# Layernorms in pairs of tiles, pieces paced by an estimate of VectorE's time, and one transfer fewer at the end, in a two-layer model kernel

## The chip, the cores and the metric

The kernel runs on one core of one Trainium2 chip. Five engines of that core matter: TensorE (PE in the profile) multiplies matrices, VectorE (DVE) and ScalarE (ACT) do elementwise work, GpSimd (POOL) does elementwise work and issues some transfers, SyncE (SP) issues the other transfers. The metric is the device time of one launch in microseconds (us); less is better.

## The reference

The input `x` is 4 x 1024 tokens of 256 numbers. Four blocks follow one another, each added to `x` behind a layernorm. All of it is float32.

```python
x = x + _layernorm(_L0_attn_ref(_layernorm(x), ...))   # gated attention in groups of 64
x = x + _layernorm(_L0_ffn_ref(_layernorm(x), ...))    # low-rank feed-forward
x = x + _layernorm(_L1_attn_ref(_layernorm(x), ...))   # 16 heads of 16, relu weights, own layernorm
x = x + _layernorm(_L1_ffn_ref(_layernorm(x), ...))    # experts choose their tokens
```

The two last ones are where the change lies:

```python
# _L1_attn_ref(x): H = 16 heads, HD = 16
w   = relu(q @ k.T / sqrt(HD))
out = (w / (sum(w) + 1e-6)) @ v
y   = x + out @ w_out + b_out
return (y - mean(y)) * rsqrt(var(y) + 1e-5) * gamma + beta
# _L1_ffn_ref(x): 8 experts, each takes the 1024 tokens with the highest gate
S    = sigmoid(xt @ Wg).T
G, I = top_k(S, 1024)
out  = (gelu(xt[I] @ W1 + b1) @ W2 + b2) * G[..., None]
new_x = zeros.at[I].add(out)
```

So one token passes four layernorms in the L1 attention: the one ahead of the projections (tag `a` in the code), the block's own with `gamma` and `beta` (tag `b`), the one around the block (tag `c`), and the one ahead of the experts' gate (tag `g`).

## The kernel before

The 4096 tokens are cut into 8 blocks of 512 (t = 0 to 7), and a block into 4 tiles of 128 tokens by 256 numbers. `xs[t]` keeps `x` of a block in on-chip memory for the whole run. The stages are the L0 layers (to 428 us), the L1 attention (428 to 1078), its tail up to the gate's logits (to 1108), the choice of tokens, the experts (1159 to 1637), and the last layernorm with its addition (to the end).

**L1 attention.** Two blocks make a row of 1024 tokens (b = 0 to 3); qh says which half of the row gives the queries. For each half there are 4 groups of heads by 8 tiles of keys, 256 steps in all. A step is `scores` (four matmuls into two single buffers and one pair buffer; relu of the singles on ACT, L1226, and of the pair on DVE, L1227) and then, from the step before, `weigh` (L1233, four matmuls that add up in `po`). The order on PE, DVE and ACT is the program's, written out by hand. Behind `weigh` stands `go_on`, which lets other work in: it takes one entry of the list `beside` (matrix work: projections of the next row, turning, output projection, gate) if there is one, and one piece of the list `rest` (vector work), two if `beside` gave something, none in the last step of a group.

**Pieces.** Vector pieces are made by `by_tile`: each layernorm is done tile by tile. `scale_of` issues statistics (bn_stats L1050, bn_aggr L1051), the addition of epsilon (L1052) and on POOL the power -1/2 (L1053). After the last group of a half `finish` turns `po` (L1265), `divide` divides by the sum of the weights (L1096 to L1106), `close` multiplies by `w_out` (`project_out`, L1121, y at L1128) and then runs for each tile: statistics of y, `affine` (L1141, L1142), statistics, `shift` (a small product on DVE at L1146, an addition on ACT at L1148), `add` (L1153), statistics, and `token_rows` (`hg`, L1164, written to `tok_d` by SP). `turn_gating` (L1177) transposes two tiles on PE; `gate` (L1191) multiplies the whole block by the gate's weights, for its two halves of 256 tokens (u = 0, 1) in two groups of 32 columns of the array, and L1199 adds to `logits`. All side products use one kind of buffer, `side`, three of them, which the two single scores of a step use too.

**Tail.** When the steps are over, `go_on` runs until both lists are empty. Then `parts` is cleared on DVE (L1308), the weights of experts 0 and 1 are loaded on SP's queue, and `sc` (L1335) starts the choice.

**End.** SP reads the experts' sums back (`back0` to `back7`). For each block `ln_stats` (L170) does four tiles' statistics on DVE and the power on POOL (L184), L1622 and L1623 make minus mean times scale on DVE and POOL, ACT applies both (L1611). For the first `ADDED` = 4 blocks, whose `x` has been written out earlier, POOL issues an accumulating transfer to the output (L1637); for blocks 4 and 5 POOL adds to `x` (L1616) and SP writes (L1617); DVE does that for blocks 6 and 7 and applies half of block 7 (L1628).

Of the kernel before, what the change touches and what calls it, by code (L numbers as in the profile page):

```python
# [9 lines left out]
F32 = mybir.dt.float32  # L10
# [3 lines left out]
ALU = mybir.AluOpType  # L14
# [34 lines left out]
ADDED = 4  # L49
# [22 lines left out]
def kernel(  # L72
# [100 lines left out]
    def ln_stats(tag, tiles):  # L173

        n = len(tiles)
        st = small.tile([P, NJ, 6], F32, tag=f"st{tag}", name=f"st{tag}")
        mv = small.tile([P, NJ, 2], F32, tag=f"mv{tag}", name=f"mv{tag}")
        for i, s in enumerate(tiles):
            nc.vector.bn_stats(st[:, i, :], s)
            nc.vector.bn_aggr(mv[:, i, :], st[:, i, :])  # L180
        ve = small.tile([P, NJ], F32, tag=f"ve{tag}", name=f"ve{tag}")
        nc.vector.tensor_scalar(ve[:, :n], mv[:, :n, 1], EPS, None, ALU.add)
        rs = small.tile([P, NJ], F32, tag=f"rs{tag}", name=f"rs{tag}")
        nc.gpsimd.tensor_tensor(rs[:, :n], ve[:, :n], mhalf[:, :n], ALU.pow)  # L184
        return mv, rs

    def layernorm(tag, dst, src):

        mv, rs = ln_stats(tag, [src[:, i, :] for i in range(NJ)])
        for i in range(NJ):  # L190
            nc.vector.tensor_scalar(
                dst[:, i, :], src[:, i, :], mv[:, i, 0:1], rs[:, i : i + 1], ALU.subtract, ALU.mult
            )

    def transpose_block(pool_ps, src, evacuate):

        for c in range(DC):
            tp = pool_ps.tile([P, NJ, P], F32, tag="tp", name="tp")
            for i in range(NJ):
                nc.tensor.transpose(tp[:, i, :], src[:, i, c * P : (c + 1) * P], ident)  # L200
            evacuate(c, tp.rearrange("p j t -> p (j t)"))
# [825 lines left out]
    with ExitStack() as st3:  # L1027
# [16 lines left out]
        def scale_of(tag, src):  # L1044

            st = small.tile([P, 6], F32, tag=f"st{tag}", name=f"st{tag}")
            mv = small.tile([P, 2], F32, tag=f"mv{tag}", name=f"mv{tag}")
            ve = small.tile([P, 1], F32, tag=f"ve{tag}", name=f"ve{tag}")
            rs = small.tile([P, 1], F32, tag=f"rs{tag}", name=f"rs{tag}")
            nc.vector.bn_stats(st, src)  # L1050
            nc.vector.bn_aggr(mv, st)  # L1051
            nc.vector.tensor_scalar(ve, mv[:, 1:2], EPS, None, ALU.add)  # L1052
            nc.gpsimd.tensor_tensor(rs, ve, mhalf[:, 0:1], ALU.pow)  # L1053
            return mv[:, 0:1], rs

        def by_tile(*steps):

            kept = {}

            def run(do, i):  # L1060
                kept[i] = do(i, *kept.get(i, ())) or ()

            return [lambda do=do, i=i: run(do, i) for do in steps for i in range(NJ)]

        def normalize(row, b, k):

            h, x = row["h"][k], xs[b * BPB + k]

            def stats(i):
                return scale_of("a", x[:, i, :])  # L1070

            def apply(i, mean, rs):
                nc.vector.tensor_scalar(h[:, i, :], x[:, i, :], mean, rs, ALU.subtract, ALU.mult)

            return by_tile(stats, apply)
# [13 lines left out]
        def divide(state, t):  # L1089
# [20 lines left out]
            return [by_weight, back]  # L1110

        def close(t, h, oT):

            y = wk.tile([P, NJ, D], F32, tag="y", name="y")

            def project_out(z):
# [11 lines left out]
                nc.vector.tensor_tensor(y[:, 2 * z : 2 * z + 2, :], pt, h[:, 2 * z : 2 * z + 2, :], ALU.add)  # L1128
                for k in range(2):
                    after(2 * z + k)  # L1130

            def after(i):
                rest.append(after_out.pop(0))
                if i == NJ - 1:
                    rest.extend(after_out)

            def stats_y(i):
                return scale_of("b", y[:, i, :])

            def affine(i, mean, rs):  # L1140
                nc.vector.scalar_tensor_tensor(y[:, i, :], y[:, i, :], mean, gam, ALU.subtract, ALU.mult)  # L1141
                nc.vector.scalar_tensor_tensor(y[:, i, :], y[:, i, :], rs, bet, ALU.mult, ALU.add)  # L1142

            def shift(i, mean, rs):
                ms = small.tile([P, 1], F32, tag="msc", name="msc")
                nc.vector.scalar_tensor_tensor(ms, mean, -1.0, rs, ALU.mult, ALU.mult)  # L1146
                x = xs[t][:, i, :]
                nc.scalar.activation(x, x, AF.Identity, bias=ms)  # L1148
                return (rs,)

            def add(i, rs):
                x = xs[t][:, i, :]
                nc.vector.scalar_tensor_tensor(x, y[:, i, :], rs, x, ALU.mult, ALU.add)  # L1153

            def stats_x(i):
                return scale_of("g", xs[t][:, i, :])

            def token_rows(i, mean, rs):
                if t < ADDED:
                    nc.sync.dma_start(out_flat[t][:, i, :], xs[t][:, i, :])  # L1160
# [5 lines left out]
                if i % 2:  # L1166
                    beside.append(lambda: turn_gating(i - 1))
# [506 lines left out]
```

## Time and profile before

| | us |
|---|---|
| median of three runs | 1675.89 (1673.42 to 1676.69) |
| the profiled execution | 1674.0 |
| its span | 1671.5 |
| relu of the pair on DVE, L1227 | 312.6 busy, 1.222 each, 256 of them |
| relu of the singles on ACT, L1226 | 278.0 busy, 0.594 each, 512 of them |
| scores on PE, L1217 | 293.6 busy |
| weighing on PE, L1233 | 274.7 busy |
| powers on POOL in the attention, L1053, 28 of tag b | 15.4 busy, 0.558 each |

The span runs from the first to the last instruction of the profiled execution; the device time holds 2.5 us more. Busy time is the sum of an engine's instructions. A line with "xN" puts N records together; the numbers after the operation are partitions by elements. In brackets stands the idle time of the engine ahead of an instruction and what ended it. "PEclk" is the clock that TensorE was granted.

### The profile page before, as it was taken

How to read it: one execution, taken by the hardware profiler on the slowest of the kernel's cores; microseconds unless marked ns; L12 is line 12 of the kernel's file. 1: busy time of each engine (PE TensorE's matmuls, PEld its weight loads, DVE VectorE, ACT ScalarE, POOL GpSimd, SP SyncE). 2: the span in 40 equal slices, each digit the busy share in tenths (PEclk: the TensorE clock that was granted, in tenths of full speed). 3: DMA queues.
4: the chain of work that ended last, by engine and by line, in shares of the span. 5: the costliest groups of instructions: out<-in, count | busy, mean ns of one | idle time of the engine just before them, and what ended most of it. 6: DMA issues, size and time to landing. Idle time of an engine off the chain costs nothing.

```text
span 1671.5 us, 22249 instructions
## 1 busy us (share of the span) xinstructions
PE 1548.5 (93%) x8663; PEld 770.4 (46%) x8663; DVE 914.9 (55%) x2046; ACT 634.6 (38%) x1099; POOL 388.1 (23%) x396
## 2 busy tenths in 40 slices
PE   7999999998999999999999999924999999999990
PEld 3666666665222232323222222202765766667670
DVE  4555556654657787878787888775121122212115
ACT  3344444534444545454545455421212122121213
POOL 4122233222201010201011101012332432433325
PEclk9999999999999999999999999955999999999995
DMA  8300000000000000000000000041233333423217
GB/s 210 107 1 1 1 1 1 1 1 1 1 1 1 14 14 13 15 13 14 14 14 1 13 5 10 8 147 26 63 66 76 68 67 71 93 46 84 32 19 208
DMA packets 66195, 64.31 MB, mean 38 GB/s; under 512 B 23181, under 2 KB 60074, under 8 KB 65962
## 3 DMA queue, kind: packets, MB, share of 16 engines
q1 hardware_dynamic: 52352, 42.81, 8.5%
q0 software_dynamic: 12864, 19.14, 6.9%
q8 instruction: 68, 1.11, 0.3%
q10 hardware_dynamic: 874, 0.93, 0.2%
q14 instruction: 37, 0.30, 0.1%
HBM read 39.64 MB, written 23.23 MB: 38 GB/s over the span
## 4 chain that ended last, share of the span: by engine, by line
PE 91%; DVE 3%; issue 3%; POOL 1%; DMA 1%; ACT 1%; SPq 0%; POOLq 0%; ACTq 0%; DVEq 0%
PE sc L1217 16%; PE po L1233 15%; PE py L1548 13%; PE ph L1526 13%; PE pg L679 3%; PE py L787 3%; PE pv L695 3%; PE pv L368 2%; PE ph L843 2%; PE po L759 2%; PE pt L1121 2%; PE pk L344 2%; PE pq L344 2%; PE pq L864 2%; PE po L763 1%
## 5 line engine op out<-in xcount | busy, mean ns | idle before, releaser
L1227 DVE TENSOR_SCALAR w<-sc 128x1024 f32<-128x1024 f32 x256 | 312.6, 1222 | 97.1 <-PE sc L1217 64.1
L1226 ACT ACTIVATE w<-sc 128x512 f32<-128x512 f32 x512 | 278.0, 594 | 229.1 <-PE sc L1217 102.5
L1217 PE MATMUL sc<-qT,kT 32*128 32x512 f32 x2048 | 293.6, 639 | 2.3 <-DVE kT L358 1.6
L1233 PE MATMUL po<-w,vaug 128*17 128x512 f32 x2048 | 274.7, 598 | 0.9 <-DVE w L1227 0.2
L1548 PE MATMUL py<-w,hid 128*128 128x256 f32 x1024 | 230.1, 380 | 0.0
L1533 ACT ACTIVATE hid<-ph,mb 128x512 f32<-128x512 f32 (+1 forms) x136 | 90.1, 662 | 365.4 <-PE ph L1526 365.4
L1526 PE MATMUL ph<-xT,w 128*128 128x512 f32 (+1 forms) x544 | 224.7, 572 | 0.5 <-DVE xT L1510 0.4
L1548 PEld LDWEIGHTS py<-w,hid 128*128 128x128 f32 x1024 | 191.1, 190 | 32.0 <-issue 7.5
L1217 PEld LDWEIGHTS sc<-qT,kT 32*128 32x128 f32 x2048 | 80.8, 183 | 186.1 <-issue 170.7
L1526 PEld LDWEIGHTS ph<-xT,w 128*128 128x128 f32 x544 | 104.6, 193 | 111.6 <-issue 107.6
L1562 POOL DMA_INDIRECT acc_d<-y,idx x64 | 101.3, 1582 | 211.5 <-issue 150.7
L1233 PEld LDWEIGHTS po<-w,vaug 128*17 128x17 f32 x2048 | 35.3, 95 | 200.0 <-issue 171.0
L1560 DVE TENSOR_TENSOR y<-py,mb 128x256 f32<-128x256 f32 x64 | 26.8, 418 | 183.9 <-PE py L1548 183.9
L1485 POOL DMA_INDIRECT got<-tok_d,idx x64 | 66.0, 1031 | 152.9 <-DVE idx L1481 135.8
L1510 DVE COPY xT<-tp 128x512 f32<-128x512 f32 (+1 forms) x34 | 22.4, 660 | 97.4 <-PE tp L1508 97.4
L1053 POOL TENSOR_TENSOR rsg<-veg,mhalf 128x1 f32<-128x1 f32 x32 | 17.8, 555 | 219.2 <-DVE veg L1052 219.2
L679 PE MATMUL pg<-nT,wh 128*128 128x512 f32 x128 | 61.6, 613 | 1.5 <-ACT nT L618 1.5
L787 PE MATMUL py<-wo,oT 128*128 128x256 f32 x256 | 61.9, 385 | 0.0
L695 PE MATMUL pv<-wh,nT 128*128 128x512 f32 x128 | 59.7, 593 | 0.0
L1481 DVE CAST idx<-parts 128x8 int32<-128x8 f32 x8 | 1.3, 167 | 101.9 <-PE parts L1479 101.9
L787 PEld LDWEIGHTS py<-wo,oT 128*128 128x128 f32 x256 | 47.3, 190 | 17.2 <-issue 9.4
L560 POOL TENSOR_TENSOR x<-x,y 128x1024 f32<-128x1024 f32 x15 | 35.3, 2353 | 75.7 <-ACT y L549 75.7
(262 smaller groups left out, 1855.0 us busy)
## 6 DMA issues: line engine op xcount, KB each, us to landing
w<-in_L_ffn_W_dram SPq DMA_DIRECT2D x16, 1024.0 KB, 5.7
x<-in_L_attn_x_dram SPq DMA_DIRECT2D x8, 512.0 KB, 5.0
acc_d<-logits SPq DMA_DIRECT2D x8, 512.0 KB, 5.1
tok_d<-hg SPq DMA_DIRECT2D x32, 128.0 KB, 1.8
back<-acc_d SPq DMA_DIRECT2D x7, 512.0 KB, 9.2
out_dram<-x SPq DMA_DIRECT2D x16, 128.0 KB, 1.7
out_dram<-back POOLq DMA_DIRECT2D x4, 512.0 KB, 6.7
out_dram<-x SPq DMA_DIRECT2D x3, 512.0 KB, 3.4
```

The source lines that it names most:

```text
L344: nc.tensor.matmul(pp, lhsT=w[:, c, t * P : (t + 1) * P], rhs=d["hT"][c], start=(c == 0), stop=(c == DC - 1))
L679: nc.tensor.matmul(pg, lhsT=wh[:, c, HID + e * P : HID + (e + 1) * P], rhs=d["nT"][:, c, :], start=(c == 0), stop=(c == DC - 1),)
L695: nc.tensor.matmul(pv, lhsT=d["nT"][:, c, i * P : (i + 1) * P], rhs=wh[:, c, 0:HID], start=(c == 0), stop=(c == DC - 1),)
L787: nc.tensor.matmul(py, lhsT=d["oT"][:, e, :], rhs=wo[:, e, :], start=(e == 0), stop=(e == EC - 1))
L1217: nc.tensor.matmul(sc, lhsT=row["kT"][t][rows, r, kt * P : (kt + 1) * P], rhs=row["qT"][rows, t, qh * TB : (qh + 1) * TB], start=True, sto ...
L1226: nc.scalar.activation(w[:, j, :], sc, AF.Relu)
L1227: nc.vector.tensor_scalar(w[:, 2:4, :], pair, 0.0, None, ALU.max)
L1233: nc.tensor.matmul(po[32 * j : 32 * j + HD + 1, :], lhsT=row["v"][:, kt, HQ * t + 2 * j + r, :], rhs=w[:, j, :], start=(kt == 0), stop=(kt ...
L1526: nc.tensor.matmul(ph, lhsT=w1[:, c, f * P : (f + 1) * P], rhs=xT[u][:, c, h * n : (h + 1) * n], start=(c == 0), stop=(c == DC - 1),)
L1533: nc.scalar.activation(hid[:, f, h * n : (h + 1) * n], ph, AF.Gelu, bias=mb1[:, e * FC + f : e * FC + f + 1])
L1548: nc.tensor.matmul(py, lhsT=hid[:, f, i * P : (i + 1) * P], rhs=w2[:, f, :], start=(f == 0), stop=(f == FC - 1),)
L1562: scatter = nc.gpsimd.indirect_dma_start(out=acc_d[:, :], out_offset=bass.IndirectOffsetOnAxis(ap=lists[e].idx[:, k : k + 1], axis=0), in_ ...
```

## The change

It does these things:

- A class `Moments` takes the statistics of several tiles at once: all bn_stats, then all bn_aggr, then one addition of epsilon and one power for all of them. In the attention a piece is a pair of tiles; `affine` centers both tiles, then scales both.
- Each piece carries an estimate of its time on VectorE. `go_on` gives 0.85 us of it in a step (twice that where `beside` gave something), carries up to 1.7 us over, and takes pieces while they fit.
- The gate runs for each pair of tiles by itself behind its turn (`gate_and_add`), one group of columns at a time, and adds 32 rows of the logits each time. The `tok_d` rows are written a pair at a time.
- The last block is closed by `at_once`, in which the instructions of the two pairs alternate. `parts` is cleared by a product with zero on ACT.
- At the end `ADDED` is 3: block 3's addition goes to POOL, and its `x` isn't written out in the attention. Block 0 is read in two equal parts. The statistics of the next block stand between those of the present one, `hand_over` comes one block later, and DVE applies half of blocks 6 and 7 and adds blocks 5, 6 and 7.

The diff, cut to its core (of rewritten functions only the new lines are shown; the old ones stand in the code above):

```diff
+ADDED = 3
...
+    class Moments:
+        def __init__(self, tag, tiles, pool=small):
+            n = len(tiles)
+            self.tiles = tiles
+            self.st = pool.tile([P, n, 6], F32, tag=f"st{tag}", name=f"st{tag}")
+            self.mv = pool.tile([P, n, 2], F32, tag=f"mv{tag}", name=f"mv{tag}")
+            self.ve = pool.tile([P, n], F32, tag=f"ve{tag}", name=f"ve{tag}")
+            self.rs = pool.tile([P, n], F32, tag=f"rs{tag}", name=f"rs{tag}")
+        def take(self, which=None):
+            for i in range(len(self.tiles)) if which is None else which:
+                nc.vector.bn_stats(self.st[:, i, :], self.tiles[i])
+        def gather(self):
+            for i in range(len(self.tiles)):
+                nc.vector.bn_aggr(self.mv[:, i, :], self.st[:, i, :])
+        def scale(self):
+            nc.vector.tensor_scalar(self.ve, self.mv[:, :, 1], EPS, None, ALU.add)
+            nc.gpsimd.tensor_tensor(self.rs, self.ve, mhalf[:, : len(self.tiles)], ALU.pow)
+        def close(self):
+            self.gather()
+            self.scale()
+        def all(self):
+            self.take()
+            self.close()
+            return self
...
+        PAIRS = (0, 2)
+        def by_pair(*steps):
+            return [(us, lambda do=do, i=i: do(i)) for us, do in steps for i in PAIRS]
...
+            def start(tag, src, i):
+                m[tag, i] = Moments(tag, [src[:, i, :], src[:, i + 1, :]])
+                return m[tag, i]
+            def center(i):
                 for k in range(2):
+                    nc.vector.scalar_tensor_tensor(
+                        y[:, i + k, :], y[:, i + k, :], m["b", i].mv[:, k, 0:1], gam, ALU.subtract, ALU.mult
+                    )
+            def affine(i):
+                for k in range(2):
+                    nc.vector.scalar_tensor_tensor(
+                        y[:, i + k, :], y[:, i + k, :], m["b", i].rs[:, k : k + 1], bet, ALU.mult, ALU.add
+                    )
+            def shift(i):
+                ms = small.tile([P, 2], F32, tag="msc", name="msc")
+                nc.vector.scalar_tensor_tensor(ms, m["c", i].mv[:, :, 0], -1.0, m["c", i].rs, ALU.mult, ALU.mult)
+                for k in range(2):
+                    nc.scalar.activation(x[:, i + k, :], x[:, i + k, :], AF.Identity, bias=ms[:, k : k + 1])
+            def add(i):
+                for k in range(2):
+                    nc.vector.scalar_tensor_tensor(
+                        x[:, i + k, :], y[:, i + k, :], m["c", i].rs[:, k : k + 1], x[:, i + k, :], ALU.mult, ALU.add
+                    )
+            def token_rows(i):
                 if t < ADDED:
+                    nc.sync.dma_start(out_flat[t][:, i : i + 2, :], x[:, i : i + 2, :])
                 if i == 0:
                     gating["h"] = wk.tile([P, NJ, D], F32, tag="hg", name="hg")
+                hg = gating["h"]
+                m["g", i].normalize([hg[:, i, :], hg[:, i + 1, :]])
+                rows = tok_d[t * TB + i * P : t * TB + (i + 2) * P, 0:D].rearrange("(j p) d -> p j d", p=P)
+                nc.sync.dma_start(rows, hg[:, i : i + 2, :])
...
+            def rows_of_half(u, n):
+                z = (t % BPB) * (TB // SEG) + u
+                return slice(32 * z, 32 * (z + n))
+            def add_logits(rows, pg):
+                nc.vector.tensor_tensor(logits[rows, :], logits[rows, :], pg[rows, :], ALU.add)
+            def gate(u, pg):
+                b, rows = t // BPB, rows_of_half(u, 1)
+                for c in range(DC):
+                    nc.tensor.matmul(
+                        pg[rows, :],
+                        lhsT=wgp[:, c, b, :],
+                        rhs=gating["hT"][:, c, u * SEG : (u + 1) * SEG],
+                        start=(c == 0),
+                        stop=(c == DC - 1),
+                    )
+            def gate_and_add(u):
                 pg = side([P, SEG], "pg")
+                gate(u, pg)
+                add_logits(rows_of_half(u, 1), pg)
+            def piecewise(z):
+                project_out(z)
+                rest.append(after_out.pop(0))
+                if z:
+                    rest.extend(after_out)
+            def gate_in_turn(i):
+                token_rows(i)
+                beside.append(lambda: turn_gating(i))
+                beside.append(lambda: gate_and_add(i // 2))
+            def at_once():
+                a, b = PAIRS
+                project_out(0)
+                ya = start("b", y, a)
+                ya.all()
+                project_out(1)
+                yb = start("b", y, b)
+                yb.take()
+                center(a)
+                yb.close()
+                affine(a)
+                center(b)
+                ca = start("c", y, a)
+                ca.take()
+                affine(b)
+                ca.close()
+                start("c", y, b).all()
+                shift(a)
+                add(a)
+                shift(b)
+                ga = start("g", x, a)
+                ga.take()
+                add(b)
+                ga.close()
+                gb = start("g", x, b)
+                gb.take()
+                gb.close()
+                pg = side([P, SEG], "pg")
+                for i in PAIRS:
+                    token_rows(i)
+                    turn_gating(i)
+                    gate(i // 2, pg)
+                add_logits(rows_of_half(0, 2), pg)
+            after_out = by_pair(
+                (1.0, lambda i: start("b", y, i).all()),
+                (1.6, lambda i: (center(i), affine(i))),
+                (1.0, lambda i: start("c", y, i).all()),
+                (0.2, shift),
+                (0.8, add),
+                (1.0, lambda i: start("g", x, i).all()),
+                (0.7, gate_in_turn),
             )
+            if t == NB - 1:
+                return [at_once]
+            return [lambda z=z: piecewise(z) for z in range(2)]
...
-        beside, rest = [], []
-        def go_on(room=1):
+        beside, rest, left = [], [], [0.0]
+        def go_on(room=0.85):
             if beside:
                 beside.pop(0)()
                 room *= 2
-            for _ in range(room):
-                if rest:
-                    rest.pop(0)()
+            left[0] = min(left[0] + room, 1.7)
+            while rest and rest[0][0] <= left[0]:
+                us, do = rest.pop(0)
+                left[0] -= us
+                do()
         state = {}
...
         parts = parts_ps.tile([P, P + NC], F32, name="parts")
-        nc.vector.memset(parts, 0.0)
         mb2 = keep.tile([P, NE, D], F32, name="mb2")
...
                 for z in range(SEGB):
                     nc.sync.dma_start(rows_d[k, z][:, :, D : D + NE], scores_t[:, k, z])
+            nc.scalar.mul(parts[:, 0:P], ident, 0.0)
...
+            for js in HALVES if t == 0 else (slice(0, NJ),):
                 read = nc.sync.dma_start(y[:, js, :], acc_t[:, js, :])
                 for scatter in last_scatters:
                     tc.add_manual_dep(read.ins, scatter.ins.name, all_rows, reason="all rows")
...
+        def apply_first_half(t):
+            y = ys[t]
+            for i in range(NJ // 2):
+                nc.vector.tensor_scalar(
+                    y[:, i, :], y[:, i, :], m[t].mv[:, i, 0:1], m[t].rs[:, i : i + 1], ALU.subtract, ALU.mult
+                )
+        def add(t, eng, js=slice(0, NJ)):
             eng.tensor_tensor(xs[t][:, js, :], xs[t][:, js, :], ys[t][:, js, :], ALU.add)
             nc.sync.dma_start(out_flat[t][:, js, :], xs[t][:, js, :])
+        def hand_over(t):
+            if t < ADDED:
+                nc.gpsimd.dma_start(out_rows[t], ys[t], accum_op=ALU.add)
+            elif t < NB - 3:
+                add(t, nc.gpsimd)
+        tiny = st5.enter_context(tc.tile_pool(name="tiny", bufs=NB))
+        m = [Moments("t", [y[:, i, :] for i in range(NJ)], tiny) for y in ys]
+        m[0].take()
         for t, y in enumerate(ys):
+            if t + 1 < NB:
+                m[t + 1].take(range(NJ // 2))
+            m[t].gather()
+            if t + 1 < NB:
+                m[t + 1].take(range(NJ // 2, NJ))
+            m[t].scale()
+            ms = tiny.tile([P, NJ], F32, tag="ms", name="ms")
+            nc.vector.tensor_scalar(ms, m[t].mv[:, :, 0], -1.0, None, ALU.mult)
+            nc.gpsimd.tensor_tensor(ms, ms, m[t].rs, ALU.mult)
+            apply_on_act(t, range(NJ) if t < NB - 2 else range(NJ // 2, NJ), ms)
+            if t:
+                hand_over(t - 1)
+        apply_first_half(NB - 2)
+        add(NB - 3, nc.vector)
+        apply_first_half(NB - 1)
+        add(NB - 2, nc.vector)
+        for js in HALVES:
+            add(NB - 1, nc.vector, js)
```

## The prediction, made before the changed kernel was run

> **What bounds the kernel now.** I read the page first: busy shares, the span in 40 slices, the chain of waits.
>
> ```profile
> span 1671.5 us, 22249 instructions
> ...
> PE 1548.5 (93%) x8663; PEld 770.4 (46%) x8663; DVE 914.9 (55%) x2046; ACT 634.6 (38%) x1099; POOL 388.1 (23%) x396
> ...
> PE   7999999998999999999999999924999999999990
> ...
> PEclk9999999999999999999999999955999999999995
> ...
> PE 91%; DVE 3%; issue 3%; POOL 1%; DMA 1%; ACT 1%; SPq 0%; POOLq 0%; ACTq 0%; DVEq 0%
> ```
>
> TensorE is the bound; only around slice 26 (1087 to 1128 us) and at the end does it stop. The change touches three stretches: L1 attention (428 to 1078 us), its tail up to the logits (to 1108), and the final layernorm (1637 to 1671.5). Windows over a quiet piece of attention, its last quarter, the tail and the end (columns: window, length, then busy time and count of PE, weight load, DVE, ACT, POOL, granted clock, DMA share, GB/s):
>
> ```profile
> 480.00:512.00 32.00, 31.95 (x252) 7.06 (x248) 20.75 (x21) 17.03 (x32) 0.00 (x0) 1.00 0.01 1
> 930.00:1078.00 148.00, 147.58 (x1096) 37.77 (x1088) 121.97 (x208) 77.58 (x144) 13.32 (x24) 1.00 0.03 9
> 1078.00:1108.00 30.00, 12.48 (x60) 6.79 (x56) 20.99 (x68) 4.59 (x10) 6.87 (x12) 0.72 0.59 205
> 1637.00:1671.50 34.50, 0.00 (x0) 0.00 (x0) 21.60 (x85) 15.50 (x30) 19.15 (x22) 0.51 0.86 244
> ```
>
> In attention PE is full even where DVE is at 82%; in the tail DVE (70%) leads; at the end PE does nothing. Then the timelines. PE around a gate step:
>
> ```profile
> 608.63 1.14 PE L1217 MATMUL sc<-qT,kT 32*128 32x512 f32 x8
> 609.71 1.05 PE L1233 MATMUL po<-w,vaug 128*17 128x512 f32 x8
> 610.58 1.03 PE L1191 MATMUL pg<-hTg,wgp 128*32 128x256 f32 x8
> 611.54 1.14 PE L1217 MATMUL sc<-qT,kT 32*128 32x512 f32 x8
> ```
>
> Score start to score start is 2.05 us in a plain step and 2.91 with the gate: anything PE is given beside the attention is paid in full. DVE, a quiet step and a crowded one:
>
> ```profile
> 506.69 1.22 DVE L1227 TENSOR_SCALAR w<-sc 128x1024 f32<-128x1024 f32 x1 [0.83 <-PE sc L1217]
> ...
> 1024.93 0.48 DVE L1141 SCALAR_TENSOR_TENSOR y<-y,mvb,gam 128x256 f32<-128x256 f32 x1
> 1025.51 0.48 DVE L1142 SCALAR_TENSOR_TENSOR y<-y,rsb,bet 128x256 f32<-128x256 f32 x1
> 1026.03 1.23 DVE L1227 TENSOR_SCALAR w<-sc 128x1024 f32<-128x1024 f32 x1
> ```
>
> DVE has 0.83 us free in a plain step. The weighing of a step starts about 3.1 us after its scores, so a relu may start some 1.6 us after the one before ended; only beyond that does PE wait. At 1026 the relu came late and the step took 3.28. I took the 255 step lengths from the score starts: 174 plain ones sum to 363.1 us, 148 of them under 2.08, and all steps together lose 9.9 us against the minimum of their kind. Tail and end:
>
> ```profile
> 1102.55 1.39 DVE L1164 TENSOR_SCALAR hg<-x,mvg,rsg 128x256 f32<-128x256 f32 x4
> ...
> 1107.72 0.42 DVE L1199 TENSOR_TENSOR logits<-logits,pg 64x256 f32<-64x256 f32 x1 [3.79 <-PE pg L1191]
> ```
>
> ```profile
> 1660.45 1.01 POOL L184 TENSOR_TENSOR rsc<-vec,mhalf 128x4 f32<-128x4 f32 x1
> 1661.55 0.20 POOL L1623 TENSOR_TENSOR msc<-msc,rsc 128x4 f32<-128x4 f32 x1
> 1661.70 2.34 POOL L1616 TENSOR_TENSOR x<-x,back 128x1024 f32<-128x1024 f32 x1
> 1664.00 1.99 POOL L184 TENSOR_TENSOR rsc<-vec,mhalf 128x4 f32<-128x4 f32 x1
> ```
>
> POOL runs without a gap from 1651.4 to 1666.3: the end is POOL's chain, then 4 us of writes.
>
> **What the Trainium skill says.** "TensorE: Matmul & The Clock Gate", Part 3: Packing small matmuls — row/col tiling, has matmuls at different tile positions run concurrently. The trace agrees: the first passes of the gate's two column groups start at 610.577 and 610.582, and eight passes take four times 0.216 us. The same page, Part 1: The HAM clock gate, halves the clock when an activity window sees an idle array. The trace shows the half clock, but 13.9 us after PE's last work (1088.2 to 1102.1), where the page gives a window of about 3.4 us; I use the 13.9. "GPSIMD Engine Reference", 1. Specifications, says POOL shares VectorE's SBUF interfaces and the two contend. The trace agrees: the same power takes 1.01 us at 1660.45, and 1.99 at 1664.00 beside VectorE's addition.
>
> **The change part by part.** Sums stand against the profiled run, 1674.0 us (span 1671.5 and 2.5 around it), 1.9 under the median of 1675.89.
>
> *Gate.* Before, both column groups run side by side, 0.86 us a block. `gate_and_add(u)` runs each alone, in a step of its own: 4 x 0.216 = 0.86 each, so 0.86 more for t = 0 to 5: 5.1 us. Block 6 now closes inside the attention (the order of instructions shows its second turn and its gates ahead of the last scores); before, they ran in the tail: one turn 0.59 and 2 x 0.86: 2.3 us. Attention +7.4 us of PE. The second logits addition is a DVE instruction of about 0.4 us, within the doubled allowance of such a step.
>
> *Stalls.* In pairs, 2 bn, 2 aggr, 1 eps cost about 1.04 us on DVE by the pitches of rows L1050 to L1052 (0.45, 0.21 and 0.07 in a chain; 0.33 and 0.10 back to back, estimated from the 0.32 of `hg` and aggr's 0.18), against 2 x 0.74 before; 0.44 saved a pair. Center+center, affine+affine take 1.6 against 1.97. In a quiet step this saves nothing: the free 0.83 hides it. What counts is where a step overflows, and larger pieces overflow differently. From the program order and those pitches: (a) the first divide (den, reciprocal, even: 1.27) falls in the plain step behind `turned`, where the two such steps before (975, 1049) lost 0.41 each; six times: +2.5. (b) After the output projections, y, two stats and two `h` share a step: about 5 x 0.55 = +2.75. (c) In the last two halves `shift` waits for POOL's power on the pair behind it (0.25 + 0.75), and its ACT additions (0.41 each) stand ahead of ACT's relus, which PE's next scores wait for: 2 x 1.75 = +3.5. (d) `turned` and four affines in one step: 2 x 0.6 = +1.2. Gone are the stalls at 1025, 953, 975, 1049 and 522: 1.23 + 0.66 + 0.82 + 0.35 = -3.06. Net +6.9. Bounds: -3 (none of a to d shows), +12 (c and b double). I take +7, with the least confidence in (c).
>
> *Tail.* Walked with the durations above from the same first y at 1084.46: y(1) 1086.2, affine a 1088.6, affine b 1090.8, shift a 1093.05, add b 1095.4, stats g to 1097.6, hg of pair a 1097.65, b 1098.65: 4.9 us before the old 1102.55. In place of one batch (eight transposes, one copy, eight passes: 5.18 us to the logits) come turn, copy, gate, turn, copy, gate in a line, about 7.1 us, with the clock at a half from about 1100 (13.9 after the projection's end): logits near 1104.75, -3.0. The clearing of `parts` leaves DVE for ACT, hidden there behind 1.7 us of idling: -0.3. Tail -3.3 (bounds -5.1, -2.0). The pairs' `tok_d` writes stand on SP between expert 1's two weight loads; expert 0 computes first, which hides that.
>
> *End.* DVE's pitch for a tile of four falls from 2.40 to about 1.83. But its first scale waits for tile 1's landing (1643.18), since the next tile's first bn pair stands ahead: 1645.1 against 1643.15. POOL then goes on as before: power 1.34, product 0.2, and 2.57 a tile with an accumulating DMA, 3.55 with an addition. With one DMA fewer and tile 3's addition more, the walk has its powers at 1645.3, 1649.7, 1652.2, 1654.8, 1658.7, 1662.2 and 1663.3; the last two have no DMA or addition between them. DVE then applies and adds tiles 5, 6, 7: x5 1664, x6 1666.1, x7 1667.9, the last write issued at 1668.55 against 1668.15, and tile 3 adds 512 KB to what SP has to write: +0.6 at 345 GB/s. End +1.0 (bounds +2; -4 if POOL kept up with DVE's 1.83). Reading tile 0 as two halves of 256 KB, not 128 and 384, moves its first bn by less than the wait for tile 1 that covers it.
>
> Sum: 7.4 + 7 - 3.3 + 1.0 = +12.1: 1686 in the profiled run's terms, 1688 in the median's; I write 1687.
>
> **The rivals.**
> *B, matrix work alone counts:* new stalls equal the old ones, 7.4 - 3.3 + 1.0 = +5: 1681. For it: 148 of 174 steps lose nothing, and DVE has less to do. Against: five of the six stalls before came from exactly such pile-ups.
> *C, ACT's queue compounds:* the shift waits of (c) also hit earlier halves, +16 to +21: 1692 to 1697. Against: earlier halves have `h` pieces between.
> *D, faster:* in the crowded steps of the attention VectorE's backlog sets the length; 8 x 0.44 us less of it in each half takes away the lost 9.9 us, and the divided gate passes fall into the time in which PE waited for relus: -9.9 - 3.3 + 1 = -12: 1664. It decides once no piece that stands ahead of a relu is longer than the 1.6 us that a relu may be late. Against: PE is busy 147.6 of 148 us in the last quarter, so a gate cannot hide.
> *E, nothing to measure:* only the old stalls go (-3), and at the end POOL, relieved of one DMA, keeps half of VectorE's better pitch (-2): 7.4 - 3 - 3.3 - 2 = -1: 1675. For it: POOL's own powers are 1.01 us where nothing disturbs them. Against: tile 3's addition takes 2.34 where the DMA took 0.91.
>
> **How the numbers follow.** Likeliest case 0.55 (1682 to 1692), B 0.20, C 0.09, E 0.09, D 0.07. Forecast 1687. The range 1676 to 1693 leaves D, half of E and most of C out. A change under 0.2% (3.35 us) can't be told from none. Faster is D and a little of E: 0.08; same, most of E and B's lower edge: 0.09; slower 0.83.
>
> **What would show it.** Gate steps of 2.9 us, 14 of them; PE busy in attention up by 7; relus on DVE or ACT over 1.6 us late at the divides and shifts; logits 3 us earlier after the last `turned`; POOL without gaps at the end. Wrong if plain steps stay at 2.05 throughout (B), or if the two gate passes overlap the weighing so that gate steps are shorter than 2.9.

## The result and the profile after

The changed kernel took 1689.91 us (median of 4 runs, 1687.75 to 1690.71) against 1676.29 of the kernel before beside it: a ratio of 1.0083, 95% interval 1.0065 to 1.0100. The forecast was 1687, range 1676 to 1693. The profiled execution took 1690.71, 16.7 more than the profiled one of before (the spans differ by 17.3), so the sums below stand against that and not against the 13.6 of the medians.

The page of the changed kernel, first lines and slices:

```profile
span 1688.8 us, 22018 instructions
...
PE 1563.6 (93%) x8663; PEld 776.3 (46%) x8663; DVE 900.5 (53%) x1979; ACT 631.2 (37%) x1098; POOL 362.8 (21%) x335
...
PE   7999999998999999999999999933999999999990
...
PEclk9999999999999999999999999955999999999995
```

VectorE, ScalarE and POOL each have less to do than before (914.9, 634.6 and 388.1 us), and the kernel is slower: the amount of their work did not set the time. PE has the same 8663 matmuls and is busy 15 us longer. Cut at the same events, the two traces differ so:

| stretch | before | after | difference | forecast |
|---|---|---|---|---|
| start to the first scores | 428.10 | 428.36 | +0.3 | 0 |
| first scores to the last turn of `po` | 651.92 | 667.38 | +15.5 | +14.4 |
| last turn to `sc`, the start of the choice | 28.49 | 27.78 | -0.7 | -3.3 |
| `sc` to the issue of the last scatter | 524.87 | 524.27 | -0.6 | 0 |
| last scatter's issue to the end of the span | 38.10 | 41.01 | +2.9 | +1.0 |
| sum | 1671.5 | 1688.8 | +17.3 | +12.1 |

The attention in windows (columns as before: busy time and count of PE, weight load, DVE, ACT, POOL, clock, DMA share, GB/s), first of the changed kernel, then of the kernel before:

```profile
428.36:1095.74 667.38, 663.97 (x4561) 188.75 (x4562) 492.05 (x809) 330.56 (x608) 55.10 (x63) 1.00 0.03 9
```

```profile
428.10:1080.01 651.91, 650.24 (x4549) 183.07 (x4550) 501.15 (x867) 332.36 (x607) 76.57 (x117) 1.00 0.03 10
```

DVE was relieved of 9 us and POOL of 21, and the stretch grew by 15.5. PE's busy time is no proof that its work grew by 14: a matmul that waits inside its group counts as busy. The lengths of the steps, from score start to score start, tell the two apart:

| kind of step | before: count, sum | after: count, sum | what changed |
|---|---|---|---|
| gate | 6, 17.46 | 14, 40.70 | 8 more, each 2.90 in place of 2.05: +6.8 |
| turn ahead of a gate | 12, 31.69 | 14, 36.97 | 2 more, +1.2, of which 0.6 stood behind the last scores before |
| turn of a projection | 12, 32.25 | 12, 34.51 | five of 3.2 in place of 2.64: +2.3 |
| output projection | 14, 57.95 | 14, 58.23 | +0.3 |
| queries and keys, values | 36, 142.98 | 36, 142.98 | nothing |
| plain, loss over 2.05 | 6.9 | 7.8, and two steps of 4.1 | +0.9 and +4.1 |

So 7.4 us are matrix work (6.8 and 0.6) and about 8 are lost time, 0.5 of it behind the last scores. The dearest lost step, on VectorE (start, duration, instruction, in brackets the idle time ahead and what ended it):

```profile
972.49 0.74 DVE L186 BATCH_NORM_STATS2 stc<-y 128x6 f32<-128x256 f32 x2
973.14 0.30 DVE L190 BATCH_NORM_AGGREGATE mvc<-stc 128x2 f32<-128x6 f32 x2
973.48 0.17 DVE L193 TENSOR_SCALAR vec<-mvc 128x2 f32<-128x2 f32 x1
973.55 0.15 DVE L1142 SCALAR_TENSOR_TENSOR msc<-mvc,rsc 128x2 f32<-128x2 f32 x1
974.52 0.16 DVE L1142 SCALAR_TENSOR_TENSOR msc<-mvc,rsc 128x2 f32<-128x2 f32 x1 [0.81 <-POOL rsc L194]
974.60 1.22 DVE L1276 TENSOR_SCALAR w<-sc 128x1024 f32<-128x1024 f32 x1
```

The same moment on ScalarE and on TensorE:

```profile
973.74 1.88 ACT L1144 ACTIVATE x<-x,msc 128x256 f32<-128x256 f32 x4 [1.44 <-DVE msc L1142]
975.53 1.55 ACT L1275 ACTIVATE w<-sc 128x512 f32<-128x512 f32 x3
```

```profile
974.12 1.12 PE L1266 MATMUL sc<-qT,kT 32*128 32x512 f32 x2
976.16 1.13 PE L1266 MATMUL sc<-qT,kT 32*128 32x512 f32 x6 [0.92 <-ACT w L1275]
```

Both shifts stand in one step, behind the statistics that the second one needs. ScalarE first waits 1.44 us for the product of the first shift, which stands behind those statistics on VectorE, and then does four additions (1.88 us) ahead of the relus; TensorE, two matmuls into the step, waits for the buffer that one of these relus must free. The next six scores start 2.0 us later. VectorE also waits 0.81 us for POOL's power, which delays its own relu. ScalarE hardly feels this: its four additions start at 973.74, 974.16, 974.72 and 975.13, so that the third comes about 0.15 us late.

The tail of the changed kernel on TensorE:

```profile
1098.59 4.97 PE L1115 MATMUL pt<-wop,oT 128*128 128x256 f32 x14 [2.27 <-DVE oT L1099]
1115.58 1.23 PE L1168 MATMUL tpg<-ident,hg 128*128 128x128 f32 x4 [12.01 <-DVE hg L207]
1117.48 1.91 PE L1186 MATMUL pg<-hTg,wgp 128*32 128x256 f32 x4 [0.67 <-ACT hTg L1171]
1119.33 1.12 PE L1168 MATMUL tpg<-ident,hg 128*128 128x128 f32 x4
1121.12 1.91 PE L1186 MATMUL pg<-hTg,wgp 128*32 128x256 f32 x4 [0.67 <-ACT hTg L1171]
```

The alternating instructions do what they were forecast to do: from the first y to the first `hg` 13.64 us pass in place of 18.08. Two things eat it. The last four lines are one chain, 7.95 us from the first `hg` to the logits in place of 5.18. And the projection took 4.97 us for work that took 3.29 before: its matmuls start 0.43 us apart up to the eighth and 0.22 after it.

### The profile page after: what moved, and what is told of

It reads as the page before. It is cut to its first block, busy times and chain, and to the rows that moved or that the text cites. A ratio compares the mean times of both kernels' runs of the same rounds, so it can differ in the third digit from the quotient of the medians.

```text
span 1688.8 us, 22018 instructions
## 1 busy us (share of the span) xinstructions
PE 1563.6 (93%) x8663; PEld 776.3 (46%) x8663; DVE 900.5 (53%) x1979; ACT 631.2 (37%) x1098; POOL 362.8 (21%) x335
## 5 line engine op out<-in xcount | busy, mean ns | idle before, releaser
L1282 PE MATMUL po<-w,vaug 128*17 128x512 f32 x2048 | 279.3, 598 | 0.8
L860 ACT ACTIVATE hid<-ph,vec 128x512 f32<-128x512 f32 x64 | 39.9, 684 | 25.4 <-PE ph L851 25.2
```

The costliest lines, as they stand in the source:

```text
L1282: nc.tensor.matmul(po[32 * j : 32 * j + HD + 1, :], lhsT=row["v"][:, kt, HQ * t + 2 * j + r, :], rhs=w[:, j, :], start=(kt == 0), stop=(kt ...
```

## The experiments

Each is an edit of the changed kernel. "Attention" is the time from the first scores to the last turn of `po`. The kernel before, run again beside each batch, took 1676.14 us (x1 to x4), 1674.31 (x5 to y2), 1673.83 (z1 to z3) and 1674.24 (z4), so runs of different batches are compared by their ratio to it.

**x1_gate: one gate for a block again (blocks 0 to 6).**

```diff
-                beside.append(lambda: gate_and_add(i // 2))
+                if i == PAIRS[-1]:
+                    beside.append(gate_both)
```

`gate_both` holds the two loops and the addition of 64 rows as before.

> The changed kernel with the gate of blocks 0 to 6 done once per block again, both column groups side by side in one step. Theory (matrix work beside the attention is paid in full): 7 blocks x 0.86 = 6.0 us less between the first scores and the last turn of po (667.4 us in the changed kernel, so about 661.4), gate steps stay at 2.9 us but only 7 of them; time near 1684. Rival (the second gate pass fell into time in which PE waited anyway): under 2 us less, time 1688 or more.

Measured: 1684.03 us (1681.86 to 1688.13), 1.0047 times the kernel before (1.0030 to 1.0064), 5.9 under the changed kernel; seven gate steps of 2.90. The attention of the profiled execution was 665.9 us, not 661: this execution, the slowest of the four, had half the clock in its first steps (2.7 us lost) and again from 976.8 to 980.2 us (1.6 lost), which is the difference. The theory holds by the gate steps and by the times, and the rival falls; since the mean clock of the four executions went from 0.961 to 0.966, the 5.9 is rough, and z3_split below repeats the test without that disturbance.

**x2_shift: the shifts in steps of their own.**

```diff
-                (0.2, shift),
+                (0.9, shift),
```

> The changed kernel with the estimate of the shift piece at 0.9 us in place of 0.2, so that the two shifts no longer share a step with the statistics they need. Theory (VectorE's wait for POOL's power, with ACT's four additions behind it, delays the relus of that step): the two steps of 4.1 us at 974 and 1050 us fall back to 2.05, 4.1 us less; time near 1686. Rival (ACT's additions alone hold the relus, the wait for POOL doesn't matter): half of it at most, since each step still carries two additions: 2 us less, time near 1688.

Measured: 1685.08 us (1684.98 to 1685.69), 1.0059 (1.0042 to 1.0076). Attention 663.95, 3.4 less; both steps of 4.1 are gone. Against the 4.1 stand a new loss of 0.4 each at 983 and 1058, where the first divide now falls in the step behind a turn as in the six halves before, and 0.15 each at 975 and 1049, where ScalarE's two additions still precede the relus; five other steps lose 0.1 each less. So the placing is the cause. The rival's forecast, that half of the 4.1 stays, falls, but not the rival itself: two additions may fit into the time by which a relu can be late and four not, and this edit takes away the wait for POOL and the second pair of additions at once. By the trace of the changed kernel, where the wait moved ScalarE's work by about 0.15 us, the additions are the larger part; no run parts the two.

**x3_pace: an account of VectorE's time with the turn and the addition of y in it.**

```diff
                 do()
+            if not rest:
+                left[0] = 0.0
...
                 nc.vector.transpose(state["turned"][:, r].rearrange("p b d -> p (b d)"), po)
+                left[0] -= 0.7
...
                 nc.vector.tensor_tensor(y[:, 2 * z : 2 * z + 2, :], pt, h[:, 2 * z : 2 * z + 2, :], ALU.add)
+                left[0] -= 0.7
```

> The changed kernel with an honest account of VectorE's time: 0.7 us is charged for the turn of po and for the addition of y, and no time is saved up while no piece waits. Theory (the late relus come from pieces let in on a budget that leaves these out): the 2.5 us steps behind the turns (6), the 3.2 us steps behind the projections (5) and the 2.7 us steps (2) fall back: 2.5 + 2.8 + 1.3 = 6.6 us less, with the first projection steps (0.41 x 6) up to 9; time 1681 to 1684. Rival (the same VectorE work makes relus late wherever it stands): the losses move to other steps, within 2 us of the changed kernel.

Measured: 1689.61 us (1688.95 to 1690.33), 1.0085 (1.0069 to 1.0102); attention 666.82. By the times the rival is right, by the steps both are. The plain steps of 2.5 and 2.7, the projections of 4.4 and the turns of 3.2 all fell back as the theory has it. But ten value steps, which had lost nothing, now took 5.1 and 4.5 in place of 3.98, and lost 8.2 us, and the two steps of 4.1 stayed, now at 980 and 1055. VectorE of this kernel in one of the ten:

```profile
553.24 0.15 DVE L1143 SCALAR_TENSOR_TENSOR msc<-mvc,rsc 128x2 f32<-128x2 f32 x1
554.14 0.16 DVE L1143 SCALAR_TENSOR_TENSOR msc<-mvc,rsc 128x2 f32<-128x2 f32 x1 [0.75 <-POOL rsc L194]
```

It is the loss of 974 again, with ScalarE's four additions from 553.43 to 555.25 ahead of the relus: the new pacing had moved both shifts, behind their statistics, into one step of every half.

**x4_end: the end of the kernel before.** The whole last stage and `ln_stats` are put back, with `ADDED = 4`, so that block 3 too is written out in the attention.

> The changed kernel with the end of the kernel before (four accumulating transfers, statistics tile by tile, block 0 read as 128 and 384 KB). Theory (the new end's first power waits until block 1 has landed, and POOL sets the pace either way): from the last scatter's issue to the end 38.1 us as before in place of 41.0, time near 1687. Rival (the new end costs nothing by itself, the reads only landed late in that execution): within 1 us of 41.0, time near 1690.

Measured: 1689.32 us (1688.91 to 1689.87), 1.0083 (1.0066 to 1.0100); from the last scatter to the end 41.1 us. The rival is right, though not for its reason: the reads landed as in the kernel before (block 1 complete 10.0 us after the last scatter's issue, 9.8 before). POOL's first accumulating transfer was late:

```profile
1659.69 1.01 POOL L184 TENSOR_TENSOR rsc<-vec,mhalf 128x4 f32<-128x4 f32 x1 [1.00 <-DVE msc L1687]
1663.27 0.97 POOL L1702 DMA_DIRECT2D out_dram<-back  x1 [2.57 <-DMA back<-acc_d]
```

The bracket names a read of the sums, but not which one. ACT had applied block 0 by 1660.8. In the kernel before the same transfer waited 0.34 us.

**x5_tail: both turns first, then one gate for the last block.**

```diff
                 for i in PAIRS:
                     token_rows(i)
                     turn_gating(i)
-                    gate(i // 2, pg)
+                for c in range(DC):
+                    for u in range(TB // SEG):
+                        nc.tensor.matmul(
+                            pg[rows_of_half(u, 1), :],
...
```

> The changed kernel with both pairs of the last block turned first and then one gate of eight matmuls, column groups side by side. Theory (the chain turn, copy, gate, turn, copy, gate in a line at half clock took 7.95 us from the first hg to the logits): the second turn no longer waits for the first copy and gate, the eight passes take 4 x 0.43 us; 5.9 us from hg to logits, 2 us less, time near 1688. Rival (hg of the second pair, not the line, sets the end): 7.5 us or more.

Measured: 1686.53 us (1685.59 to 1690.79), 1.0080 (1.0065 to 1.0096); 4.79 us from the first `hg` to the logits, 3.2 less: the theory, and more. The ratio is that of the changed kernel within its interval, so the times alone do not show the gain. Its gate in the trace of this run took 2.13 us for eight passes, the clock coming back to full in it, which the estimate of 5.9 did not have (in y2_all, at half clock throughout, the same chain takes 5.32):

```profile
1115.39 2.22 PE L1168 MATMUL tpg<-ident,hg 128*128 128x128 f32 x8 [12.00 <-DVE hg L207]
1117.55 2.13 PE L1244 MATMUL pg<-hTg,wgp 128*32 128x256 f32 x8
```

**x6_awake: TensorE kept busy during the last divide.**

```diff
         finish(*before)
+        awake = side([P, 4, P], "awake")
+        for k in range(12):
+            nc.tensor.transpose(awake[:, k % 4, :], ident, ident)
         while beside or rest:
```

> The changed kernel with 12 transposes of the identity that nobody reads, put on TensorE behind the last weighing, so that its pause during the last divide shrinks from 2.3 to about 0.5 us. Theory (that pause lets the clock fall to a half at 1099, so that the output projection takes 5.0 us in place of 3.3): from the last turn of po to the first y 4.45 us in place of 5.74, time 1.3 us lower. Rival (the clock falls for another reason, or the pause must only be shorter than the kernel before's 2.29): 5.4 to 5.8 us again.

Measured: 4.45 us from the last turn to the first y, and every projection matmul 0.22 after the one before: the theory's number. 1687.03 us (1686.07 to 1693.28), 1.0084 (1.0065 to 1.0104). The times do not show it: the ratio is that of the changed kernel. In the profiled execution 1.0 us came back between `sc` and the last scatter (525.27, 524.27 in the changed kernel), where the clock returned to full 55.8 us after `sc` in place of 53.7; tail and choice together are 1.5 us shorter.

**y1_att: x1, x2 and x3 together.**

> The changed kernel with the three edits to the attention together: one gate a block, shifts at 0.9 us, and time charged for turn and y. Theory (each removes losses of its own, and what the charging alone moved into the value steps was again a shift beside its statistics): attention 667.4 - 6.0 - 3.4 - 8 = 650 us, under the 651.9 of the kernel before; time near 1673. Rival (the losses of the charging alone stay in the value steps): attention 657 or more, time near 1680.

Measured: 1669.74 us (1669.01 to 1673.96, 20 runs), 0.9978 of the kernel before (0.9971 to 0.9984). Attention 648.64 us, under the estimate; all steps together lose 4.6 us (9.9 before). The value steps are back at 3.98: the theory, and the rival falls. The parts do not add up, they need each other: x3's account is worth 0.6 us alone, and 648.64 against 667.38 - 6.0 - 3.4 = 658.0 is 9.4 us beside x2's shift.

**y2_all: y1 with x5 and x6.**

> The attention edits, the joined last gate and the transposes behind the last weighing together. Theory: 650 us of attention, then 24 us from the last turn to the scores of the choice (28.5 before); with an end that is no shorter, 1669 to 1671, faster than both kernels. Rival (parts don't add up): 1675 or more.

Measured: 1666.75 us (1665.23 to 1670.11), 0.9957 (0.9944 to 0.9971): faster than both kernels, and 3.0 us under y1_att in the same batch, which is what x5 and x6 bring together. Attention 648.62, tail 23.52.

**z1_first: at the end, block 0's statistics closed before block 1's are begun** (on top of y2_all).

```diff
-            if t + 1 < NB:
+            if 0 < t < NB - 1:
                 m[t + 1].take(range(NJ // 2))
...
+            if t == 0:
+                m[1].take()
```

> The kernel with all edits (y2_all), and at the end block 0's statistics closed before any of block 1's are begun. Theory (the new end starts late because block 0's scale stands behind a read of block 1): from the last scatter's issue to POOL's first power about 9.5 us in place of 12.1, and since POOL is the bound the last power comes earlier by 1.5 to 2.5 us too; time near 1665. Rival (POOL's second power and the first transfer wait for later reads and for ACT anyway): the first power earlier, the last one within 0.5 us of 30.1.

Measured: POOL's first power 9.85 us after the last scatter's issue (12.09), its last one at 29.95 (30.12). The rival is right: the end takes 39.9 us (40.1 in y2_all), time 1665.38 (1664.88 to 1666.24), 0.9952 (0.9936 to 0.9969), which the intervals do not tell from y2_all. The late start of the new order costs the end nothing here.

**z2_oldend: y2_all with the end of the kernel before.**

> The kernel with all edits (y2_all) and the end of the kernel before. Theory (the old end takes 38.1 us from the last scatter's issue to the end of the span as in the kernel before, and the 41.1 of x4_end came from a first transfer that was issued 2.5 us late in that one execution): 38 to 39 us against 40.2 of y2_all, time 1 to 2 us lower. Rival (the old end is no better, and its 38.1 was luck): 40 us or more, time equal or higher.

Measured: 40.6 us from the last scatter to the end, and 1668.74 us (1664.79 to 1670.35, 14 runs), 0.9963 (0.9955 to 0.9971). The rival again; POOL's first transfer waited 2.50 us, as in x4_end. So the 2.5 us was no accident of one execution. Eight of the fourteen executions had a mean clock of 0.963 to 0.965 and took 1668.2 to 1670.4 us, the other six 1664.8 to 1666.5, so the median says little about the end; the profile and the six speak against a gain of more than about 1 us. The profiled execution had half the clock in its first attention steps, as x1_gate's did (attention 651.34).

**z3_split: y2_all with the gate in two again.**

> The kernel with all edits (y2_all), but the gate of blocks 0 to 6 split in two again, one group of columns at a time. Theory (its price is matrix work alone, also where relus are no longer late): attention 648.6 + 7 x 0.86 = 654.6 us, 14 gate steps of 2.90, time 6 us higher. Rival (in the changed kernel part of it came with late relus): 652 us or less.

Measured: 1672.46 us (1671.42 to 1676.76, 12 runs), 0.9995 (0.9986 to 1.0003), 5.7 over y2_all (6.4 by the ratios). Attention 653.87, 5.3 more: 13 gate steps of 2.90 in place of 7, and the fourteenth behind the last scores. 0.86 us a gate, with no late relus around it: the theory, and the rival falls.

**z4_vadd: z1_first with block 4's addition on VectorE.**

```diff
-            elif t < NB - 3:
+            elif t < NB - 4:
                 add(t, nc.gpsimd)
...
+        add(NB - 4, nc.vector)
         apply_first_half(NB - 2)
```

> The kernel with all edits and the early first statistics (z1_first), and block 4's addition at the end moved from POOL to VectorE, ahead of block 6's application. Theory (POOL sets the end: each addition costs it 2.34 us, and VectorE stands idle for 3.9 us before POOL's last powers): the last power starts 1.3 to 2.3 us earlier than 30.0 us after the last scatter's issue, and the end 1 to 2 us earlier; time near 1664. Rival (VectorE's addition slows POOL's powers by as much, as 2.00 against 1.01 us showed): the last power within 0.5 us of 30.0, time near 1665.5.

Measured: POOL's last power 28.07 us after the last scatter (29.95), end at 37.6 (39.9), 1663.75 us (1663.23 to 1664.18): 0.9937 of the kernel before (0.9923 to 0.9950). POOL of this kernel at its end:

```profile
1649.10 1.02 POOL L194 TENSOR_TENSOR rst<-vet,mhalf 128x4 f32<-128x4 f32 x1
1650.20 0.78 POOL L1723 TENSOR_TENSOR ms<-ms,rst 128x4 f32<-128x4 f32 x1
1650.93 1.00 POOL L194 TENSOR_TENSOR rst<-vet,mhalf 128x4 f32<-128x4 f32 x1
1652.02 0.20 POOL L1723 TENSOR_TENSOR ms<-ms,rst 128x4 f32<-128x4 f32 x1
1652.17 1.08 POOL L194 TENSOR_TENSOR rst<-vet,mhalf 128x4 f32<-128x4 f32 x1
```

Three powers follow each other without an addition between the last two. The rival falls. That POOL sets the end is shown here by taking work off it; taking DVE's wait off (z1_first) did nothing that could be measured.

## Why the prediction was right, and where it was not

**Gate, +7.4: right.** 14 steps of 2.90 and two turns: 7.4 measured. Taking the split out (x1_gate, 5.9 in time) and putting it in (z3_split, 5.7) agree with 7 x 0.86, so rival D, that passes fall into waiting time, is out. The sign "PE busy in attention up by 7" was no good one: it rose by 13.7, since a waiting matmul counts as busy.

**Stalls, +7: right in sum, about +8.** (a) six divides behind turns: 2.5 us steps, 0.4 each, as forecast. (b) five turns of 3.2: 2.8 against 2.75. (c) two shifts: 4.1 against 3.5, the term with the least confidence; x2_shift brings it to 0.3 by placing alone. The place was forecast rightly, the make-up of the price not: 1.0 us a time was put down to the wait for POOL's power, which moved ScalarE's work by some 0.15; the rest, 0.75, is less than two additions of 0.41, and four stood ahead of the relus. (d) two of 2.7: 1.3 against 1.2. The old stalls named as gone are gone. Rivals B (new stalls equal the old ones) and E (only the old ones go) are out by 8 and more; rival C's mechanism exists, but in x3_pace, where shifts met their statistics in every half.

**Tail, -3.3: wrong in size, -0.7.** The walk to `hg` holds: 4.9 forecast, 4.4 measured, 4.8 where the clock stayed full (13.30 us in x1_gate and y1_att). The chain from `hg` to the logits was put at 7.1 with the clock at a half and took 7.95 so (7.96 in x1_gate and y1_att). The logits came 0.4 us earlier after the last turn, where 3 was the sign. The term that was missing is the clock in the pause of the last divide: +1.3; x6_awake shows that a pause of 2.27 had brought the half clock. Here the prediction misread its trace. It took the half clock to come 13.9 us after the last work; in the kernel before it began at 1091.44, 3.1 us after the last matmul ended at 1088.32, and 13.9 is nearer to the time for which TensorE then stood idle (14.79). The same pause stood in the kernel before and cost nothing there, because of where it fell (see the last section), so part of this miss was chance.

**End, +1.0: wrong in size, +2.9 by the profile, not shown by the times.** POOL as the bound was right (z4_vadd). The first power came 3.0 us later than before, 1.9 forecast, because block 1's read completed 11.1 us after the last scatter in place of 9.8; POOL's chain to the last power was 2.6 us shorter, and 2.5 (about 1.7 in the forecast) went after it to VectorE's longer queue of applications and additions. z1_first shows that the late first power is not what counts. The new end took 39.4 to 41.0 us in the nine traces that have it unchanged, so 2.9 is also the upper edge of its spread. The old end put back gains nothing clear (x4_end 0.6 us, z2_oldend none), so the new end cannot be charged with 2.9. Why the first accumulating transfer is 2.5 us late when the old end stands behind the changed attention, and not in the kernel before, stays open.

The forecast of 1687 was 3 us low in the medians. The attention's two terms were each within a microsecond or so, and the misses in tail and end point the same way: the range held without misses that cancel, but its upper half was needed.

## What to carry to other kernels

Where one engine is full, less work on another buys nothing by its amount; only where an instruction stands ahead of what the full engine waits for does it count, and grouping makes such pieces longer. Here two pieces in one slot, behind the statistics that the second one needed, put four additions ahead of the relus, and this one placing undid nearly all that better pacing had gained (x3_pace: 8.2 us lost, 0.6 left as gain). A time budget for side work must charge everything that runs in that slot, on the other engines too: the budget of this kernel counts VectorE's time alone. Two matrix products that use different columns of the array belonged in one place; splitting them cost 0.86 us each time.

## What the runs showed of the hardware

The granted clock reacts to shorter pauses than the kernel before had shown, and where a pause falls decides. In each of the fourteen traces the moments at which the granted clock changes stand whole multiples of 3.413 us apart. Cut along this grid around the last divide, the changed kernel and then the kernel before show (the last three columns are clock, DMA share and GB/s):

```profile
1095.30:1098.71 3.41, 1.14 (x6) 0.41 (x4) 2.66 (x5) 0.00 (x0) 0.00 (x0) 1.00 0.00 0
1098.71:1102.13 3.42, 3.42 (x9) 2.71 (x10) 0.65 (x1) 0.00 (x0) 0.00 (x0) 0.50 0.00 0
```

```profile
1081.20:1084.61 3.41, 1.75 (x8) 1.57 (x9) 1.69 (x4) 0.00 (x0) 0.00 (x0) 1.00 0.00 0
1084.61:1088.03 3.42, 3.29 (x20) 2.01 (x18) 2.92 (x9) 0.59 (x1) 0.33 (x1) 1.00 0.34 96
1088.03:1091.44 3.41, 0.29 (x2) 0.00 (x0) 3.13 (x12) 0.00 (x0) 2.00 (x4) 1.00 0.94 328
1091.44:1094.85 3.41, 0.00 (x0) 0.00 (x0) 3.03 (x10) 0.00 (x0) 0.00 (x0) 0.50 0.99 376
```

In the changed kernel the pause lies whole in one window, and the next window has half the clock; in the kernel before only 1.66 us of it lie in one window, and the clock stays. The pause in the last divide, 2.3 us long, brought half the clock in five of eight executions without the extra transposes: in these five (the changed kernel, x2 to x5) 1.98 to 2.27 us of it lay in one window, in the other three (before, x1_gate, y1_att) at most 1.51 to 1.70. With the transposes, which left a pause of 1.0, it did in none of six. Over all fourteen traces, each of the 65 windows at full clock in which TensorE was busy for less than 42% was followed by half the clock, and of the windows above 44% only three were (of five between, two).

Two of these three, busy for 54%, hold a pause of 1.56 us ahead of the first scores of the L1 attention, which cost the attention about 2.7 us in one (z2_oldend 651.34 against 648.62). In the other twelve traces the same pause lies in one window too and costs nothing; why these two fell stays open, and so does the third (x1_gate, 73%, ahead of 976.8 us).

```profile
430.00:432.00 2.00, 1.52 (x5) 0.51 (x6) 1.03 (x1) 2.00 (x5) 1.20 (x1) 0.53 0.00 0
432.00:434.00 2.00, 2.00 (x10) 0.15 (x8) 0.57 (x1) 0.77 (x2) 1.15 (x1) 0.50 0.03 8
434.00:436.00 2.00, 2.00 (x12) 0.52 (x8) 1.70 (x6) 0.00 (x0) 0.19 (x1) 0.50 0.00 0
436.00:438.00 2.00, 2.00 (x16) 0.13 (x8) 0.65 (x1) 0.78 (x2) 0.52 (x1) 0.76 0.00 0
```

These are windows of z2_oldend. The Trainium skill ("TensorE: Matmul & The Clock Gate", Part 1: The HAM clock gate) says that the activity window runs freely, so that the moment of a change depends on where in it the work falls. The traces agree, with their grid of 3.413 us. The page puts the half clock down to at least one idle window of some 3.4 us; here a window with a pause of 2.0 to 2.3 us was enough, and the measurement decides.

VectorE can be held up by POOL without waiting for a result of it, as one place suggests: in z1_first a VectorE instruction of 512 elements, 0.15 us elsewhere, took 2.04. It started inside POOL's addition of 2.34 us and ended with it (1648.61 and 1648.58):

```profile
1646.57 2.04 DVE L193 TENSOR_SCALAR vet<-mvt 128x4 f32<-128x4 f32 x1
1646.24 2.34 POOL L1698 TENSOR_TENSOR x<-x,back 128x1024 f32<-128x1024 f32 x1
```

"GPSIMD Engine Reference", 1. Specifications, names contention for the shared memory interfaces with VectorE instructions that run in a two-port mode or have two inputs in that memory. VectorE's instruction here has one input; in which mode it ran, no run shows.
